# Perceiver block on one core: where the sums of the keys' squares stand, and in which tiles of TensorE they are made

## The chip, the core and the metric

The kernel runs on one core of one Trainium2 chip. The metric is the device time of one launch in microseconds (us). Five engines work on queues of their own: TensorE (PE in the profile, its weight loads PEld), VectorE (DVE), ScalarE (ACT), GpSimd (POOL) and SyncE (SP), which issues the DMAs. They wait for each other by semaphores.

## What is computed

Everything is float32. `x` has 128 rows of 512. Three residual steps follow each other: cross attention of `x` to a context of 12544 rows (16 heads of 32), self attention with block-scaled weights (16 heads of 128), and a mixture of 32 experts with a shared one. The change lies in the first step, cut here to what matters:

```python
def rms_norm(x, w, eps=1e-6):
    return x * jax.lax.rsqrt(jnp.mean(x * x, axis=-1, keepdims=True) + eps) * w

q     = rms_norm(linear(x, q_w, q_b), norm_q_w)
k     = rms_norm(linear(ctx_txt, k_w, k_b), norm_k_w)         # ctx_txt: rows 257 and on
v     = linear(ctx_txt, v_w, v_b)
k_img = rms_norm(linear(ctx_img, k_img_w, k_img_b), norm_k_img_w)   # ctx_img: rows 0 to 256
v_img = linear(ctx_img, v_img_w, v_img_b)
out = linear(attention(q, k, v) + attention(q, k_img, v_img), o_w, o_b)
```

A key is divided by the root of the mean of its 512 squares. The weight `norm_k_w` is folded into the queries, and the factor of one key, called `rinv` in the kernel, is applied to its scores.

## The kernel before

**Blocks and tiles.** The context is cut into 25 blocks. Block 0 is the image part (257 rows in tiles of 86, 86 and 85), blocks 1 to 24 are the text part with 512 rows each (511 in the last) in four tiles of 128. A tile is numbered `t`, its place in its block `j` (0 to 3). The text before and after says "pass j" for the work done at tile j.

**Software pipeline.** While the tiles of block b are attended to, keys and values of block b+1 are made by `step(b + 1, k)`, k from 1 to 7. These are the seven products of Strassen's scheme in Winograd's form for the keys (`kp`) and for the values (`vp`), each of eight matmul records of 128x256 (line 1078; a float32 matmul shows as two records). Their sums of context halves (`xs`) are made by GpSimd in `ctx_sums` (lines 1060 to 1063). Steps 1 and 2 share a bank of PSUM, as do 5 and 3, and 7 and 4. Three banks (pool `ps_a`) serve all these products and the `ssq` tiles below in turn.

**Per tile** the main loop (line 1523) does the following, and `pin` keeps each engine's instructions in the order of the program:

- `scores(t, "b")`: 16 matmuls in four groups of 32 rows into the four banks of `sb` (line 1162)
- `weights`: VectorE makes p = sb * rinv - maximum in one instruction over 128x2048 (line 1251), ScalarE its exponential (line 1259)
- `weigh_pending`: the 16 matmuls of the tile before, weights times values, in four groups of 32 columns (`av_new`, line 1268)
- `into_sums`: GpSimd adds the weights of the tile before to `ls` (line 1426), one instruction over 128x2048

**The squares.** When step 3 has filled the first half of a block's keys, ScalarE squares it (`squares(b, 0)`, line 1117), and GpSimd adds the four chunks of 128 channels into one by two instructions (`add_squares(b, 0)`, line 1123). Step 4 fills the second half, treated by `add_squares(b, 1)`. `key_norms(b, [0, 1])` and `key_norms(b, [2, 3])` then finish the sums for two tiles each: one matmul per tile with the squares as weights and a single column of ones (`ssq`, line 1015), one small VectorE instruction (`ms`, line 1025) and one power of -1/2 by GpSimd (`rinv`, line 818 through `inv_sqrt`).

**Order in a block of the main loop before the change**, for block b (what the change touches is in bold):

| pass | PE ahead of the scores | GpSimd | PE after `weigh_pending` |
|---|---|---|---|
| 0 | step 1 of b+1, **ssq of tiles 0 and 1 of b** | **rinv**, ls, squares (half 1) of b | step 2 |
| 1 | step 6, **ssq of tiles 2 and 3 of b** | **rinv**, ls | |
| 2 | step 5, step 7 of the keys | ls (and a weight scaling in six blocks) | step 3 |
| 3 | step 7 of the values | ls, **squares (half 0) of b+1**, xs of b+2 | step 4 |

The last block (24) has a sequence of its own from line 1628 on, and so have blocks 0 and 1, which end in a short loop over three tiles at line 1442. Between that loop and the main one GpSimd adds two small tensors (`x0ob`, `vbs`, lines 1467 and 1469).

Of the kernel before, what the change touches and what calls it, by code (L numbers as in the profile page):

```python
# [20 lines left out]
XH, XHD = 16, 32  # L21
# [749 lines left out]
def fast_block(ctx: ExitStack, tc: tile.TileContext, a: dict, out: bass.AP, amiss: bass.AP):  # L771
    nc = tc.nc
# [13 lines left out]
    ones = const.tile([P, P], FP, tag="ones", name="ones")  # L786
# [51 lines left out]
    def pin(ins):  # L838

        return tc.keep_in_program_order(ins)  # L840
# [55 lines left out]
    with ExitStack() as xs:  # L896
# [24 lines left out]
        m = -(-IMG // 3)  # L921
# [7 lines left out]
        NB, NT = len(blocks), len(tiles)  # L929
# [53 lines left out]
        sq = {}  # L983
# [26 lines left out]
        def key_norms(b, js):  # L1010

            ts = [blocks[b][3][j] for j in js]
            sp = bank(f"ssq_{b}_{js[0]}")
            for j, (o, m) in enumerate(ts):
                pin(nc.tensor.matmul(  # L1015
                    sp[:m, j : j + 1],
                    lhsT=sq[b][:, 0, o : o + m],
                    rhs=ones[:, 0:1],
                    start=True,
                    stop=True,  # L1020
                ))
            ms = small.tile([P, 4], FP, tag="ms", name=f"ms_{b}_{js[0]}")
            t0 = tile0[b] + js[0]
            for j0, j1, m in row_groups(ts):
                pin(nc.vector.tensor_scalar(  # L1025
                    ms[:m, j0:j1], sp[:m, j0:j1], 1.0 / D, 1e-6, ALU.mult, ALU.add
                ))
                pin(inv_sqrt(rinv[:m, t0 + j0 : t0 + j1], ms[:m, j0:j1]))
# [90 lines left out]
        def add_squares(b, i):  # L1119

            ks = slice(i * HALF, (i + 1) * HALF)
            for w in (2, 1):
                pin(nc.gpsimd.tensor_tensor(  # L1123
                    sq[b][:, :w, ks], sq[b][:, :w, ks], sq[b][:, w : 2 * w, ks], op=ALU.add
                ))
# [269 lines left out]
        m = heights[1]  # L1395
# [41 lines left out]
        def weigh_pending():  # L1437
            k, pk = pend
            weigh(k, pk, k in (t1, SWITCH), k == SWITCH - 1)


        for t in range(t1 + 1, tile0[2]):
            p, s = weights(t)
            j = t - t1
            if j == 1:
                largest(t, s)
                step(2, 6)
            elif j == 2:
                step(2, 5, "v")
                largest(t, s)  # L1450
            else:
                step(2, 7)
                largest(t, s)
                ctx_sums(3)
            weigh_pending()
            if j == 1:
                step(2, 5, "k")
            elif j == 2:
                step(2, 3)
            else:  # L1460
                step(2, 4)
            into_sums(*pend)
            if j == 2:
                add_squares(2, 0)
            pend = (t, p)
# [57 lines left out]
        for t in range(tile0[2], tile0[LAST]):  # L1523
            b, part, o, m = tiles[t]
            j = t - tile0[b]


            make = step
            if t == SWITCH + 3:
                pin(nc.tensor.matmul(  # L1530
                    avp["txt"].rearrange("p g q -> p (g q)"),
                    lhsT=ident,
                    rhs=kept["av"],
                    start=False,
                    stop=False,
                    skip_group_check=True,
                ))
            late = make if b + 1 < LAST else (lambda *of: None)
            if j == 0:
                make(b + 1, 1)  # L1540
                key_norms(b, [0, 1])
            elif j == 1:
                make(b + 1, 6)
                key_norms(b, [2, 3])
            elif j == 2:
                make(b + 1, 5)
                late(b + 1, 7, "k")
            else:
                late(b + 1, 7, "v")
            if t == tile0[LAST] - 1:  # L1550
                unsummed = pend
            else:
                into_sums(*pend)
            if j == 0:
                add_squares(b, 1)
            elif j == 2 and b in AHEAD:
                scale_weights((b - AHEAD[0]) // 3, "qkv"[(b - AHEAD[0]) % 3], nc.gpsimd)
            elif j == 3:
                add_squares(b + 1, 0)
                if b + 2 < NB:  # L1560
                    ctx_sums(b + 2)
            if t == SWITCH:
                m_bc["txt"] = m_new
            p, s = weights(t)
            weigh_pending()
            pend = (t, p)
            if t == tile0[RENEWED + 1]:
                m_new = xc.tile([P, 4, CHUNK], FP, tag="mx", name="mb_new")
                on_all(q_new, m_new, "new")
                pin(nc.vector.tensor_tensor(over, q_new, q_old, ALU.subtract))  # L1570
                less = small.tile([P, XH], FP, tag="less", name="less")
                pin(nc.scalar.activation(less, over, AF.Exp, scale=-1.0))
            elif t == tile0[RENEWED + 1] + 1:

                shrink = rowp.tile([P, D], FP, tag="h", name="shrink")
                on_heads(less, shrink, "less")
            elif t == SWITCH:
                av_old = avp["txt"].rearrange("p g q -> p (g q)")
                kept = {"av": row("kept_av", "kept_av")}
                pin(nc.vector.tensor_tensor(kept["av"], av_old, shrink, ALU.mult))  # L1580
                avp["txt"] = ps_o.tile([P, NC, P], FP, tag="o", name="av_new")
            elif t == SWITCH + 2:
                lp = bank("l_old")
                for i in range(4):
                    r = slice(i * XHD, (i + 1) * XHD)
                    pin(nc.tensor.matmul(
                        lp[r, :], lhsT=ones[:, :XHD], rhs=ls_old[i // 2][:, i % 2, :],
                        start=True, stop=True, skip_group_check=True,
                    ))
                kept["l"] = row("kept_l", "kept_l")  # L1590
                pin(nc.vector.tensor_tensor(kept["l"], lp, shrink, ALU.mult))
            if j == 2:
                make(b + 1, 3, "k")
            if b <= RENEWED:
                largest(t, s)
            if j == 0:
                make(b + 1, 2)
            elif j == 2:
                make(b + 1, 3, "v")
            elif j == 3:  # L1600
                late(b + 1, 4)
                if b + 3 < NB:
                    load_ctx(b + 3)
            if t == tile0[RENEWED + 1] - 1:
                q_new = query_max(mx, P, "t1")
            if b == RENEWED + 3 and j == 0:
                pin(nc.vector.reciprocal(l_img, l_img))
            if b == RENEWED + 3 and j == 1:
                flat = att_img.rearrange("p g q -> p (g q)")
                pin(nc.vector.tensor_tensor(flat, flat, l_img, ALU.mult))  # L1610
            if b == RENEWED + 3 and j == 2:
                pin(nc.gpsimd.tensor_tensor(
                    att_img, att_img, vbs.unsqueeze(2).to_broadcast([P, NC, P]), op=ALU.add
                ))
            if b == AHEAD[0] - 2 and j == 0:
                for t_, nm in ((bq, "bq"), (bk, "bk"), (gw, "gate_w")):
                    pin(nc.sync.dma_start(out=t_, in_=a[nm]))
                pin(nc.sync.dma_start(out=gb, in_=a["gate_bias"].partition_broadcast(P)))
                homes[2] = slot(xc, "mb", "q")
                load_codes(2, "q", homes[2][0])  # L1620
                load_codes(2, "k", homes[2][1])
            if b == AHEAD[0] - 1 and j == 0:
                for g in range(2):
                    for nm, t in zip("qkv", homes[g]):
                        load_codes(g, nm, t)
                    load_scales(g, aw.tile([P, 3 * GW], FP, tag="sc", name=f"sc_{g}"))

        b, t = LAST, tile0[LAST]
# [1 line left out]
        bo = rowp.tile([P, D], FP, tag="h", name="bo")  # L1630
        k, p = pend
        s = scores(t, "b")
        key_norms(b, [0, 1])
        ps = [weights(t, s, xc.tile([P, 4, CHUNK], FP, tag="vw", name="p_last"))[0]]
        step(b, 7, "k")
        step(b, 4, "k")
# [222 lines left out]
    for g in range(NG):  # L1859
# [17 lines left out]
        if g:  # L1877
            o = gather(g - 1)
# [35 lines left out]
    for q in range(4):  # L1914
        for k in range(4):
            j = 4 * q + k
            pin(nc.tensor.matmul(  # L1917
                yp,
                lhsT=aoT[:, j, :],
                rhs=wo[q][k // 2][:, k % 2 * D : k % 2 * D + D],  # L1920
                start=(j == 0),
                stop=(j == SH - 1),
# [351 lines left out]
    sp = {}  # L2274
# [175 lines left out]
```

## Time and profile before

| what | value |
|---|---|
| median of three runs | 1094.71 us (1092.88 to 1095.63) |
| the profiled execution, its own time | 1091.79 us |
| its span in the profile | 1090.1 us |
| granted clock of TensorE | 0.997 |
| PE busy | 1064.8 us (98%), 10464 matmul records |
| GpSimd busy | 691.0 us (63%) |
| VectorE, ScalarE busy | 545.6 us (50%), 356.1 us (33%) |
| one block of the main loop | 34.10 us |

The page shows the busy time of each engine, the span in 40 slices, and the chain of work that ended last, followed back from the end. The chain of waits gives the time that one step adds between its neighbours; the timeline gives start and length of each run of like instructions, where a matmul's length includes its passage through the array, so that lengths of neighbours overlap. "128*32" means weights with 128 rows and 32 columns.

### The profile page before, as it was taken

How to read it: one execution, taken by the hardware profiler on the slowest of the kernel's cores; microseconds unless marked ns; L12 is line 12 of the kernel's file. 1: busy time of each engine (PE TensorE's matmuls, PEld its weight loads, DVE VectorE, ACT ScalarE, POOL GpSimd, SP SyncE). 2: the span in 40 equal slices, each digit the busy share in tenths (PEclk: the TensorE clock that was granted, in tenths of full speed). 3: DMA queues.
4: the chain of work that ended last, by engine and by line, in shares of the span. 5: the costliest groups of instructions: out<-in, count | busy, mean ns of one | idle time of the engine just before them, and what ended most of it. 6: DMA issues, size and time to landing. Idle time of an engine off the chain costs nothing.

```text
span 1090.1 us, 23595 instructions
## 1 busy us (share of the span) xinstructions
PE 1064.8 (98%) x10464; PEld 844.3 (77%) x10464; DVE 545.6 (50%) x668; ACT 356.1 (33%) x438; POOL 691.0 (63%) x374
## 2 busy tenths in 40 slices
PE   8999999999999999999999999999999899999996
PEld 6778888888888888888888888888888669754332
DVE  3676864574445544455444554445544568441110
ACT  2353333333333333333333333333333324303111
POOL 2256886887878778787787888889888600000000
PEclk9999999999999999999999999999999999999999
DMA  9221021101111011110124201111010499519995
GB/s 307 90 79 41 2 88 40 41 1 40 40 40 41 2 40 40 40 41 2 40 82 165 59 2 40 40 40 40 1 41 1 141 390 368 174 72 413 384 414 234
DMA packets 43247, 113.17 MB, mean 104 GB/s; under 512 B 6720, under 2 KB 12032, under 8 KB 42112
## 3 DMA queue, kind: packets, MB, share of 16 engines
q1 hardware_dynamic: 43136, 111.57, 28.2%
q8 instruction: 84, 1.38, 0.5%
q14 instruction: 27, 0.22, 0.1%
HBM read 111.26 MB, written 0.29 MB: 102 GB/s over the span
## 4 chain that ended last, share of the span: by engine, by line
PE 89%; DVE 3%; DMA 3%; POOL 2%; ACT 1%; issue 1%; SPq 0%; DVEq 0%; ACTq 0%; POOLq 0%
PE kp L1078 27%; PE vp L1078 25%; PE sb L1162 10%; PE av_new L1268 8%; PE up L2075 4%; PE acc L2062 2%; PE ssq L1015 1%; PE qp L1759 1%; PE kp L1759 1%; PE yp L1917 1%; PE svp L1780 1%; PE vp L1230 1%; DMA h<-in_experts 1%; DMA wo<-in_experts 1%; DMA wv<-in_experts 1%; DVE p L1251 1%
## 5 line engine op out<-in xcount | busy, mean ns | idle before, releaser
L1426 POOL TENSOR_TENSOR ls<-ls,p 128x2048 f32<-128x2048 f32 x81 | 369.1, 4556 | 38.2 <-ACT p L1259 36.6
L1259 ACT ACTIVATE p<-p 128x2048 f32<-128x2048 f32 (+1 forms) x95 | 179.9, 1893 | 462.1 <-DVE p L1251 461.9
L1251 DVE SCALAR_TENSOR_TENSOR p<-sb,rinv,mb_new 128x2048 f32<-128x2048 f32 (+1 forms) x86 | 199.9, 2325 | 59.2 <-PE sb L1162 59.2
L1123 POOL TENSOR_TENSOR sq<-sq 128x512 f32<-128x512 f32 x96 | 96.2, 1002 | 33.1 <-ACT sq L1117 29.3
L1162 PE MATMUL sb<-qT_txt,kraw 32*128 32x128 f32 (+1 forms) x3040 | 111.5, 283 | 1.5 <-DVE p L1251 1.5
L1162 PEld LDWEIGHTS sb<-qT_txt,kraw 32*128 32x128 f32 (+1 forms) x3040 | 93.4, 186 | 19.6 <-issue 17.1
L1078 PE MATMUL kp<-xs,w_k_w 128*128 128x256 f32 x384 | 95.4, 392 | 0.0
L1078 PE MATMUL kp<-ctx,w_k_w 128*128 128x256 f32 x384 | 93.3, 386 | 0.0
L1078 PE MATMUL kp<-xs,kt 128*128 128x256 f32 x384 | 92.7, 385 | 0.1
L1268 PE MATMUL av_new<-p,v 128*32 128x128 f32 (+1 forms) x2720 | 92.5, 276 | 0.0
L1078 PE MATMUL vp<-vt,xs 128*128 128x256 f32 x384 | 91.1, 380 | 1.1 <-ACT kraw L1106 1.1
L1078 PE MATMUL vp<-w_v_w,xs 128*128 128x256 f32 x384 | 90.9, 380 | 0.0
L1078 PE MATMUL vp<-w_v_w,ctx 128*128 128x256 f32 x384 | 90.8, 380 | 0.0
L818 POOL TENSOR_TENSOR rinv<-ms,neghalf 128x2 f32<-128x2 f32 (+4 forms) x51 | 39.6, 778 | 71.2 <-DVE ms L1025 71.2
L1078 PEld LDWEIGHTS kp<-xs,kt 128*128 128x128 f32 x384 | 73.6, 193 | 11.4 <-POOL wk L1426 0.4
L1078 PEld LDWEIGHTS kp<-xs,w_k_w 128*128 128x128 f32 x384 | 69.3, 190 | 16.3 <-issue 8.9
L1078 PEld LDWEIGHTS vp<-vt,xs 128*128 128x128 f32 x384 | 72.8, 190 | 11.4 <-ACT kraw L1106 1.6
L1078 PEld LDWEIGHTS kp<-ctx,w_k_w 128*128 128x128 f32 x384 | 70.9, 190 | 13.7 <-issue 5.3
L1078 PEld LDWEIGHTS vp<-w_v_w,xs 128*128 128x128 f32 x384 | 72.9, 190 | 10.0
L1078 PEld LDWEIGHTS vp<-w_v_w,ctx 128*128 128x128 f32 x384 | 72.9, 190 | 9.8
L1268 PEld LDWEIGHTS av_new<-p,v 128*32 128x32 f32 (+1 forms) x2720 | 69.6, 110 | 11.2 <-issue 1.2
L818 POOL TENSOR_TENSOR rs_x<-ve_x,neghalf 128x1 f32<-128x1 f32 x3 | 1.7, 551 | 101.2 <-DVE ve_x L826 101.2
(441 smaller groups left out, 1470.4 us busy)
## 6 DMA issues: line engine op xcount, KB each, us to landing
ctx<-in_ctxT SPq DMA_DIRECT2D x23, 1024.0 KB, 4.9
wo<-in_experts SPq DMA_DIRECT2D x20, 512.0 KB, 9.9
wo<-in_wo_codes SPq DMA_DIRECT2D x8, 512.0 KB, 6.9
wq<-in_experts SPq DMA_DIRECT2D x8, 512.0 KB, 9.8
wk<-in_experts SPq DMA_DIRECT2D x8, 512.0 KB, 9.2
wv<-in_experts SPq DMA_DIRECT2D x8, 512.0 KB, 9.2
q<-in_experts SPq DMA_DIRECT2D x8, 512.0 KB, 9.4
f<-in_experts SPq DMA_DIRECT2D x8, 512.0 KB, 9.7
```

The costliest lines, as they stand in the source:

```text
L818: return nc.gpsimd.tensor_tensor(dst, src, neghalf[:m, :n], op=ALU.pow)
L1015: pin(nc.tensor.matmul(sp[:m, j : j + 1], lhsT=sq[b][:, 0, o : o + m], rhs=ones[:, 0:1], start=True, stop=True,))
L1078: pin(nc.tensor.matmul(t[:, h, :], lhsT=lhs, rhs=rhs, start=(first and h == 0 and c == 0), stop=(h == 1 and c == 1), skip_group_check=True,))
L1123: pin(nc.gpsimd.tensor_tensor(sq[b][:, :w, ks], sq[b][:, :w, ks], sq[b][:, w : 2 * w, ks], op=ALU.add))
L1162: pin(nc.tensor.matmul(s[:m, i, g * P : (g + 1) * P], lhsT=kraw[b][rows, g, o : o + m], rhs=qT[part][rows, g, :], start=True, stop=True,))
L1251: pin(nc.vector.scalar_tensor_tensor(p[:m, k : k + n], s[:m, k : k + n], rinv[:m, t : t + 1], m_bc[part][:m, k : k + n], ALU.mult, ALU.sub ...
L1259: pin(nc.scalar.activation(p[:m, k : k + n], p[:m, k : k + n], AF.Exp))
L1268: pin(nc.tensor.matmul(avp[part][i * XHD : (i + 1) * XHD, g, :], lhsT=vv[b][:m, t - tile0[b], hd * XHD : (hd + 1) * XHD], rhs=p[:m, i, g * ...
L1426: pin(nc.gpsimd.tensor_tensor(d, d, src, op=ALU.add))
L1759: pin(nc.tensor.matmul(pp[:, k, :], lhsT=w[:, c, k * SHD : (k + 1) * SHD], rhs=hT2[:, c, :], start=(c == 0), stop=(c == NC - 1),))
L2062: pin(nc.tensor.matmul(acc, lhsT=lhsT, rhs=rhs, start=(n_acc == 0), stop=last))
L2075: pin(nc.tensor.matmul(up[r : r + m, :], lhsT=lhsT, rhs=w13_of((kind != "all", i), c), start=(c == 0), stop=(c == NC - 1), skip_group_chec ...
```

## The change

The sums of squares of a tile are made by four matmuls, each with 32 columns of the weights into 32 rows of PSUM, in place of one with 128 columns. Both calls of `key_norms` of a block now stand after `weigh_pending`: that of tiles 2 and 3 still in pass 1, that of tiles 0 and 1 in pass 3 of the block before. For the latter `add_squares(b + 1, 0)` is moved ahead of `into_sums` of pass 3 on GpSimd. Block 2's first call moves to the last pass of the short loop, the last block's first call from its own sequence to the main loop. The calls of blocks 0 and 1 and the last block's second call stay where they are, in the new form.

```diff
@@ key_norms
             for j, (o, m) in enumerate(ts):
-                pin(nc.tensor.matmul(
-                    sp[:m, j : j + 1],
-                    lhsT=sq[b][:, 0, o : o + m],
-                    rhs=ones[:, 0:1],
-                    start=True,
-                    stop=True,
-                ))
+
+                for r in range(0, m, XHD):
+                    r1 = min(r + XHD, m)
+                    pin(nc.tensor.matmul(
+                        sp[r:r1, j : j + 1],
+                        lhsT=sq[b][:, 0, o + r : o + r1],
+                        rhs=ones[:, 0:1],
+                        start=True,
+                        stop=True,
+                        skip_group_check=True,
+                    ))
@@ short loop over the tiles of block 1
             weigh_pending()
+            if j == 3:
+                key_norms(2, [0, 1])
@@ main loop
             if j == 0:
                 make(b + 1, 1)
-                key_norms(b, [0, 1])
             elif j == 1:
                 make(b + 1, 6)
-                key_norms(b, [2, 3])
...
+            if j == 3:
+                add_squares(b + 1, 0)
             if t == tile0[LAST] - 1:
                 unsummed = pend
             else:
                 into_sums(*pend)
...
-            elif j == 3:
-                add_squares(b + 1, 0)
-                if b + 2 < NB:
-                    ctx_sums(b + 2)
+            elif j == 3 and b + 2 < NB:
+                ctx_sums(b + 2)
...
             p, s = weights(t)
             weigh_pending()
+            if j == 1:
+                key_norms(b, [2, 3])
+            elif j == 3:
+                key_norms(b + 1, [0, 1])
@@ last block
         s = scores(t, "b")
-        key_norms(b, [0, 1])
```

## The prediction

> **What bounds the kernel now.** I read the page first (busy time by engine), then the groups by shape, the chain of waits through one block, and the timeline of single instructions.
>
> ```profile
> PE 1064.8 (98%) x10464; PEld 844.3 (77%) x10464; DVE 545.6 (50%) x668; ACT 356.1 (33%) x438; POOL 691.0 (63%) x374
> ```
>
> ```profile
> L1268 PE MATMUL av_new<-p,v 128*32 128x128 f32 x2688 | 90.8, 276 | 0.0
> ...
> L1015 PE MATMUL ssq<-ones,sq 128*128 128x1 f32 x190 | 24.2, 231 | 0.8 <-POOL sq L1123 0.8
> ```
>
> In the main loop PE is never idle: over one block (520.6 to 554.7) its busy time is 34.10 of 34.10 us. So what a step adds on PE is what it costs, and the chain of waits gives that (columns: start, us, what):
>
> ```profile
> 520.42 0.34 PE ssq L1015 x4
> 520.75 1.10 PE sb L1162 x32
> 521.86 1.01 PE av_new L1268 x32
> 522.87 1.92 PE kp L1078 x8
> ```
>
> A call of key_norms for two tiles is four records and 0.34 us. A check without the chain: the scores of tiles 0, 1 and 2 start at 520.68, 530.24 and 537.73. The first distance, 9.56 us, holds 32 product records and one call, the second, 7.49, 24 records and none; eight records are 1.73 in the chain, so the call is 9.56 - 7.49 - 1.73 = 0.34. How the two forms run shows in the timeline (start, length of the whole run, engine, shape, count):
>
> ```profile
> 520.04 0.63 PEld L1015 LDWEIGHTS ssq<-ones,sq 128*128 128x128 f32 x4
> 520.25 0.50 PE L1015 MATMUL ssq<-ones,sq 128*128 128x1 f32 x4
> ```
>
> ```profile
> 521.79 0.16 PEld L1268 LDWEIGHTS av_new<-p,v 128*32 128x32 f32 x8
> ```
>
> ```profile
> 521.79 0.32 PE L1268 MATMUL av_new<-p,v 128*32 128x128 f32 x4
> ```
>
> A full load lasts 190 ns, one of 32 columns 110: 80 ns for 96 columns, so 0.83 ns a column, 107 ns for 128 and 27 for 32. Today's call is four loads of 107 of which the first lies under the product ahead: 3 x 0.107 = 0.32 of the 0.34. It is bound by loads, not by its single column. The av_new rows show what side by side means: eight loads of 110 ns end within 0.16 us, so they start within 0.05; four matmuls of 0.297 us end within 0.32, so they start within 0.02, some 7 ns apart.
>
> **The change part by part.** *The matmuls.* 44 calls (blocks 2 to 23, two each) leave the place ahead of the scores: -0.34 each. Each comes back after av_new as 16 pairs of load and matmul in the tile form in which av_new runs, so with no change of form ahead of it; the change to the full array behind it is paid today as well (kp after av_new: 1.92 against 1.73). Call the new price x. In each of four column groups there are four loads of 27 ns; the first hides under av_new's last stream as today's hides under vp; 3 x 27 plus the spread of 7 ns over four groups is 0.11. Ends: 0.10, and 16 times av_new's own pace (1.01/32 = 31.6 ns) = 0.51, an upper end because that pace streams 128 columns. I take 0.13, near the load rows, because the call of today is load-bound in the same sense. 44 x (0.13 - 0.345) = -9.5.
>
> Here a rule speaks against the change. The Trainium skill (TensorE: Matmul & The Clock Gate, section "Wait — 56ns, not 53.3ns?") says that starts of matmuls never come closer than about 25 ns however few columns stream, and its page TensorEngine Tiling (Array Packing), section "Instruction Overhead", advises not to tile a dimension that is small already, as one column costs like 60. By it x = 16 x 25 = 0.40, and the matmuls would give 44 x 0.055 = +2.4 in place of -9.5. The row above has four starts within 0.02 us, so the floor does not hold between column groups; whether it holds for 16 in a row no run here shows, since av_new's bursts pause for their streams. I follow the row, and keep 0.40 as a case.
>
> *What waits behind the new place.* The bank of tiles 2 and 3 is reused by step 7 (kp at 535.7), which now waits for ms; ms stands behind p on VectorE: 531.55 + 2.35 + 0.15 = 534.05, 1.6 us early. The bank of tiles 0 and 1 is reused by step 1 (550.68): p 546.53 + 2.35, ms at 549.04, also 1.6 early. The rinv of tiles 2 and 3 now stands behind the ls of pass 1, ends near 534.6 and is read at 539.04. All cost nothing; with less cover each 0.1 us would cost 2.2 in 22 blocks. No DMA is moved, and none is issued by these steps; SP's order stays.
>
> *GpSimd's order in pass 3*, the one place without cover:
>
> ```profile
> 543.24 1.04 ACT L1117 ACTIVATE sq<-kraw 128x1024 f32<-128x1024 f32 x1
> 543.48 4.54 POOL L1426 TENSOR_TENSOR ls<-ls,p 128x2048 f32<-128x2048 f32 x1 [2.73 <-ACT p L1259]
> ...
> 547.98 2.10 POOL L1123 TENSOR_TENSOR sq<-sq 128x512 f32<-128x512 f32 x2
> ...
> 555.18 0.70 POOL L818 TENSOR_TENSOR rinv<-ms,neghalf 128x2 f32<-128x2 f32 x1
> ...
> 556.12 2.35 DVE L1251 SCALAR_TENSOR_TENSOR p<-sb,rinv,mb_new 128x2048 f32<-128x2048 f32 x1 [1.07 <-PE sb L1162]
> ```
>
> From 543.48 to 555.88 GpSimd runs 12.40 us without a gap, and rinv is ready just ahead of p. With the squares first it cannot start before ScalarE's squares end, 544.28 (+0.08 as at 849.42 to 849.50 in the last block). The sums are then ready at 546.45, 0.9 us before av_new of pass 3 ends (547.34): PE does not wait for them. But rinv ends at 544.36 + 12.40 = 556.76, and p waits for it. What follows from a late rinv is in the trace already, at the start of block 2, where x0ob stands ahead of it:
>
> ```profile
> 108.52 0.66 POOL rinv L818
> ...
> 109.21 2.36 DVE p L1251
> ...
> 111.59 1.91 ACT p L1259
> 113.50 0.73 ACT kraw L1106 x2
> ...
> 114.28 1.99 PE vp L1078 x8
> ```
>
> vp of step 6 takes the bank that ScalarE's kraw frees, 5.07 us after p starts; there PE lost 1.15 us. In the loop: 556.76 + 0.04 + 5.07 = 561.87 is the earliest vp, less the 0.345 - x that PE gained in pass 1 ahead of those squares: 561.525 + x. PE alone would be there at 527.87 + 34.10 - 2(0.345 - x) = 561.28 + 2x. So PE stalls by 0.245 - x, 0.115 at x = 0.13, in 20 of the 22 blocks (the first two have longer VectorE stages): +2.3.
>
> *Edges.* At the start of block 2 rinv now stands ahead of ls, x0ob and vbs, so its stall goes: -1.15 (next late: ls, which has some 2 us before its p buffer is due). In the last block the path runs through the call:
>
> ```profile
> 853.53 0.55 PE ssq L1015 x4
> 854.10 0.17 DVE ms L1025
> ...
> 854.34 0.71 POOL rinv L818
> 855.08 2.36 DVE p_last L1251
> ```
>
> With rinv made before (squares 851.6, ms behind p at 852.5, rinv 853.2), p_last starts at the end of the scores, 853.6: -1.5; what is late next is the scores, which wait for the p before them. The last block's second call stays behind av_new: -0.2. Blocks 0 and 1 pay for changes of tile form between full-array work, about +0.2 (kp's 0.19) each where PE is on the path: +0.3.
>
> Sum: -9.5 + 2.3 - 1.15 - 1.5 - 0.2 + 0.3 = -9.7 us. Made against the profiled execution, 1091.8 (span 1090.1), it gives 1082.1; that run lies 2.9 under the median, so of the median 1094.7 it is 1085.0. Two runs' difference of about 0.3%, 3.3 us, is what the measurement can tell.
>
> **The rivals.**
> 1. *Sixteen small pairs run at av_new's sustained pace* (slower). If 31.6 ns is a limit of issuing and not of streaming 128 columns, x = 0.51: 44 x 0.16 = +7.0, edges -2.2, so +4.9: 1099.6. Decided at x = 0.40, where the loop's loss equals the edges' gain. For: nothing in the trace has more than eight short starts in a row. Against: starts 7 ns apart, and bursts of four with 0.11 us pauses, the length of a stream. Chance 0.12.
> 2. *The floor of 25 ns*, x = 0.40: +0.1, so 1094.8, no change. Chance 0.13.
> 3. *GpSimd's chain binds more than the rows add up to*: if rinv comes 0.3 later still, the loop gains 0.43 - 0.415 and the edges remain, about -2.3: 1092.4. For: the stall of block 2 is the same chain. Chance 0.10.
> 4. *x between*, about 0.25, with a pass of the same column group waiting for the one ahead: no stall, 44 x -0.095 = -4.2, edges -2.4: 1088.1. Chance 0.20.
> 5. *The forecast* with x from 0.10 to 0.17 (-10.5 to -8.8, or -12 if the stall does not appear). Chance 0.45.
> That the squares are still made ahead of the scores by a scheduler is no rival: the order of the built program puts eight ssq matmuls behind av_new on PE.
>
> **How the numbers follow.** The likeliest is 5: 1085.0. The low end is its no-stall case, 1082; the high end takes in 3 and most of 2: 1095. Faster by over 0.3%: 5, 4 and a third of 3, 0.68; within 0.3%: most of 2 and the rest of 3, 0.19; slower: 1 and a little of 2, 0.13.
>
> **What would show it.** Right: ssq in the chain near 0.1 us after av_new; kp after it still about 1.9; a block of 33.8; PE idle ahead of vp some 0.1 us with kraw as releaser; VectorE's p of pass 0 waiting for rinv; no p waiting for rinv near 109. Wrong: ssq at 0.4 or more, or kp behind it above 2.2; ssq waiting for GpSimd's sq; a block of 34.1 or longer with PE idle ahead of vp.

## The result and the profile after

| | before | after |
|---|---|---|
| median, us | 1094.79 (5 runs, 1092.88 to 1095.63) | 1080.82 (5 runs, 1080.05 to 1082.35) |
| ratio | | 0.9878, 95% interval 0.9865 to 0.9891 |
| profiled execution: own time, span | 1091.79, 1090.1 | 1080.82, 1079.1 |

The kernel became 14.0 us faster; the prediction was 1085.0, from 1082 to 1095. The direction and the mechanism were right, but the gain was larger than forecast: the time lies 1.2 us under the low end, so the prediction missed. With the later runs there are 46 of before, median 1093.5 (1091.85 to 1096.45), and 9 of after, median 1080.8: against this larger sample the gain is 12.7 us.

The page's busy times of after, and its groups by shape:

```profile
PE 1054.4 (98%) x11052; PEld 826.1 (77%) x11052; DVE 540.9 (50%) x668; ACT 356.0 (33%) x438; POOL 689.7 (64%) x374
```

```profile
L1272 PE MATMUL av_new<-p,v 128*32 128x128 f32 x2688 | 90.8, 276 | 0.0
...
L1018 PE MATMUL ssq<-ones,sq 128*32 128x1 f32 x778 | 13.9, 170 | 1.7 <-POOL sq L1127 1.7
```

PE has 588 records more and is busy for 10.4 us less: in a call of `key_norms`, 16 small pairs of a weight load and a matmul cost less than 4 large ones. (Lines have moved by 3 or 4: 1015 is now 1018, 1251 is 1255, 1268 is 1272.)

The chain of waits through a block (start, us, what) shows the call of `key_norms` behind av_new:

```profile
505.01 1.10 PE sb L1166 x32
506.12 0.99 PE av_new L1272 x30
507.11 0.11 PE ssq L1018 x15
507.22 1.92 PE kp L1082 x8
...
521.82 1.80 PE vp L1082 x8
```

av_new and ssq together take 1.10 us where av_new alone took 1.01; kp behind them takes 1.92 as before. vp of step 6 takes 1.80 in place of 1.73: that is the stall that was predicted. Its cause is in the timeline (start, length, engine, what; in brackets the engine's idle time before it and its releaser):

```profile
504.11 2.07 POOL L1127 TENSOR_TENSOR sq<-sq 128x512 f32<-128x512 f32 x2 [3.96 <-ACT sq L1121]
506.14 4.56 POOL L1430 TENSOR_TENSOR ls<-ls,p 128x2048 f32<-128x2048 f32 x1
...
515.82 0.70 POOL L818 TENSOR_TENSOR rinv<-ms,neghalf 128x2 f32<-128x2 f32 x1
...
516.55 2.35 DVE L1255 SCALAR_TENSOR_TENSOR p<-sb,rinv,mb_new 128x2048 f32<-128x2048 f32 x1 [4.95 <-POOL rinv L818]
```

GpSimd waits for ScalarE's squares, then runs without a gap, and p of pass 0 waits for its rinv.

The two waits for rinv at the edges are gone. First the chain at the start of block 2, where vp now follows kp at once, then in the last block, where p_last follows the scores (before, it came at 855.08, behind ssq, ms and rinv, while the scores had started at 852.36):

```profile
111.31 1.73 PE kp L1082 x8
113.04 0.02 issue
113.06 1.99 PE vp L1082 x8
...
842.07 1.22 PE sb L1166 x32
...
843.38 0.06 DVE p_last L1255
```

Where the time went, from the starts of the scores and of later matmuls in both traces:

| stretch | before, us | after, us | difference |
|---|---|---|---|
| start to the scores of tile 7 | 105.57 | 105.48 | -0.09 |
| tile 7 to 11 (block 2) | 37.71 | 36.07 | -1.65 |
| tile 11 to 19 | 70.53 | 69.47 | -1.06 |
| tile 19 to 91, 18 blocks | 613.74 | 606.43 | -7.31 (-0.406 each) |
| tile 91 to 95 | 24.80 | 24.62 | -0.18 |
| tile 95 to the output projection | 30.00 | 28.05 | -1.95 |
| from there to the gate's matmul | 83.49 | 83.49 | 0.00 |
| gate to the end | 124.22 | 125.48 | +1.26 |

All that the change touches gives -12.24 us. A second profile of the changed kernel gives only -11.35 up to the output projection: in block 3 VectorE waits 1.36 us there for the landing of a small DMA (`shrink`), and PE 0.81 us behind it. That DMA belongs to both kernels and lands late in five of the twelve profiles, the split at the old place among them, so such an account is good to about 1 us. The last row has the experts' transfers; other profiles show below how far it moves by itself.

### The profile page after: what moved, and what is told of

Its sections match the earlier page's. It is cut to its first block, busy times and chain, and to the rows that moved or that the text cites. A ratio compares the mean times of both kernels' runs of the same rounds, so it can differ in the third digit from the quotient of the medians.

```text
span 1079.1 us, 24731 instructions
## 1 busy us (share of the span) xinstructions
PE 1054.4 (98%) x11052; PEld 826.1 (77%) x11052; DVE 540.9 (50%) x668; ACT 356.0 (33%) x438; POOL 689.7 (64%) x374
## 4 chain that ended last, share of the span: by engine, by line
PE 91%; DMA 3%; DVE 3%; issue 1%; ACT 1%; POOL 0%; SPq 0%; DVEq 0%; ACTq 0%
PE kp L1082 28%; PE vp L1082 26%; PE sb L1166 10%; PE av_new L1272 8%; PE up L2082 4%; PE acc L2069 2%; PE qp L1766 1%; PE kp L1766 1%; PE yp L1924 1%; PE svp L1787 1%; PE vp L1234 1%; DMA wv<-in_experts 1%; DMA wo<-in_experts 1%; DMA h<-in_experts 1%; PE av_old L1272 1%
## 5 line engine op out<-in xcount | busy, mean ns | idle before, releaser
L1121 ACT ACTIVATE sq<-kraw 128x1024 f32<-128x1024 f32 x48 | 50.0, 1042 | 12.1 <-DVE kraw L1112 12.1
```

Source lines behind the costliest of these rows:

```text
L1121: pin(nc.scalar.activation(sq[b][:, :, ks], kraw[b][:, :, ks], AF.Square))
```

## The experiments

**The split alone.** It is made at the old place ahead of the scores; the rest is as before.

```diff
-                pin(nc.tensor.matmul(
-                    sp[:m, j : j + 1],
-                    lhsT=sq[b][:, 0, o : o + m],
+                for r in range(0, m, XHD):
+                    r1 = min(r + XHD, m)
+                    pin(nc.tensor.matmul(
+                        sp[r:r1, j : j + 1],
+                        lhsT=sq[b][:, 0, o + r : o + r1],
```

> The kernel before with its ssq matmuls split into four groups of 32 columns, at the old place ahead of a tile's scores; GpSimd's order is the old one. Theory A (the price of a call is its loads, plus a change of tile form where its neighbours have another form): a call costs 0.10 us as after av_new, plus a change of form on one side that the full-array call did not pay there, some 0.1 to 0.19 us (0.19 is what kp pays behind av_new, 1.92 against 1.73). So 0.20 to 0.29 us a call in place of 0.345, a block of 33.8 to 34.0 us, 44 calls give -6.4 to -2.4 us, and no edge of the other parts: 1088.4 to 1092.4. Theory B (the split alone does it, the place is indifferent): 0.10 a call, 44 x -0.245 = -10.8: about 1084. Theory C (the place does it, the split is worth nothing): 0.34 a call, 1094.8.

Measured 1089.76 us, ratio 0.9956 (0.9942 to 0.997) to the kernel before, measured beside it, as in all that follow. The chain of waits:

```profile
516.79 1.73 PE vp L1082 x8
518.52 0.24 PE ssq L1018 x16
518.75 1.10 PE sb L1166 x32
```

A call takes 0.24 in place of 0.34, a block 33.89. That is theory A's range: the split alone brings 0.10 a call, and the place is not indifferent.

**The place alone.** The changed kernel with the 128-column matmul of before.

```diff
-                for r in range(0, m, XHD):
-                    r1 = min(r + XHD, m)
-                    pin(nc.tensor.matmul(
-                        sp[r:r1, j : j + 1],
-                        lhsT=sq[b][:, 0, o + r : o + r1],
+                pin(nc.tensor.matmul(
+                    sp[:m, j : j + 1],
+                    lhsT=sq[b][:, 0, o : o + m],
```

> The changed kernel with the ssq matmuls of 128 columns on the whole array, as before, but at the new places behind av_new, and with GpSimd's new order. Theory A: three loads of 107 ns stand open, 0.32 us, and the change of form (0.19) moves from kp to ssq, so ssq with kp costs 0.34 more than kp alone, as today: the loop gains nothing from PE, no stall ahead of vp (0.245 - 0.345 is below nothing), and the edges stay (block 2 about -1.2, last block about -1.9): 1091 to 1092, block 34.10 us. Theory C (the place does it): near 1082. A form change that is paid twice would show as ssq above 0.45 or kp still at 1.92 behind it, and 1095 or more.

Measured 1093.49 us, ratio 1.0 (0.9992 to 1.0009), between theory A's 1092 and the 1095 of a form change that is paid twice. The chain of waits:

```profile
531.87 1.01 PE av_new L1268 x32
532.88 0.54 PE ssq L1015 x4
533.42 1.83 PE kp L1078 x8
```

ssq and kp take 2.37, kp alone 1.92, so the call costs 0.45 here, and a block is 34.31. My theory was off by 0.11, one load of 107 ns: behind av_new the first full load is not covered either. By single records the four loads start 0, 108, 217 and 329 ns behind the first, and kp's first load 441 ns behind it. The new place alone is worse for the loop; what its edges give (block 2, the last block) pays for most of that, -3.1 us against +4.2 in this trace.

Taken from the lengths of blocks, the four prices of a call of two tiles are:

| us a call | ahead of the scores | behind av_new |
|---|---|---|
| 128 columns | 0.345 | 0.453 |
| four groups of 32 | 0.243 | 0.105 |

The two parts do not add up: the move costs 0.11 with the old form and gains 0.14 with the new one.

**GpSimd's old order.** The changed kernel, with the squares' sums of pass 3 behind ls.

```diff
-            if j == 3:
-                add_squares(b + 1, 0)
             if t == tile0[LAST] - 1:
...
-            elif j == 3 and b + 2 < NB:
-                ctx_sums(b + 2)
+            elif j == 3:
+                add_squares(b + 1, 0)
+                if b + 2 < NB:
+                    ctx_sums(b + 2)
```

> The changed kernel with GpSimd's old order in pass 3 alone: the squares of the first half are added up behind the sums of the weights (ls, 4.54 us) instead of ahead. Theory A: ls starts when p's exponentials are there, some 0.6 us ahead of ScalarE's squares, the squares are then done about 2.7 us after av_new of pass 3 has ended, and PE, whose ssq stands behind av_new, waits that long in some 21 blocks: +50 to +60 us against the changed kernel, near 1135, and PE's idle time in front of ssq names GpSimd's sq. Theory D (GpSimd's order is free because PE's queue has slack): within 3 us of the changed kernel.

Measured 1177.51 us, ratio 1.076 (1.0738 to 1.0781): 96.7 us over the changed kernel, far over both theories. PE's waits (engine, line, releaser: us in total, times, longest) give the part that was foreseen:

```profile
PE ssq L1018 <- POOL sq L1127: 56.4, 22, 2.9
```

Two of the 22, 1.7 us together, stand at calls outside the loop, at 55 us and in the last block, as in the changed kernel. The other 20 are 2.73 us each. The rest is in the chain behind one of these waits, and in the busy times by stretch (stretch, its length, then the engines' busy times; the third last column is the granted clock):

```profile
594.81 0.39 PE ssq L1018 x16
595.21 3.71 PE kp L1082 x8
598.91 2.90 PE vp L1082 x8
```

```profile
594.80:598.90 4.10, 4.09 (x25) 3.36 (x26) 0.16 (x1) 0.70 (x1) 3.94 (x4) 0.50 0.02 4
598.90:601.80 2.90, 2.90 (x10) 2.36 (x9) 0.88 (x2) 1.06 (x1) 2.90 (x3) 0.61 0.00 0
601.80:612.00 10.20, 10.20 (x103) 8.64 (x102) 3.04 (x2) 4.25 (x6) 6.29 (x4) 1.00 0.70 216
```

kp takes 3.71 in place of 1.92 at a granted clock of 0.50. The trace has 0.50 behind 18 of the 20 waits, for 3.4 us behind 12 of them and for 6.8 us behind six, of which this is one; behind the first two waits (135 and 210 us) the clock stayed at 1.00. A block is 38.68, 4.99 more than in the changed kernel: 2.73 of waiting and some 2.25, on average, of what follows it, nearly all of it the slow array. So the third part of the change, four moved lines on GpSimd, is what makes the new place usable at all.

**rinv ahead of the context sums.** The changed kernel with xs of pass 3 behind the call of `key_norms`.

```diff
-            elif j == 3 and b + 2 < NB:
-                ctx_sums(b + 2)
...
             elif j == 3:
                 key_norms(b + 1, [0, 1])
+                if b + 2 < NB:
+                    ctx_sums(b + 2)
```

> The changed kernel with the four sums of the context (xs, 4.8 us on GpSimd) of pass 3 behind the reciprocal roots of the next block's first tiles instead of ahead of them. Theory A (the late rinv delays p of pass 0, that ScalarE's kraw, that the bank of vp of step 6: 0.07 to 0.08 us a block): rinv is ready some 4 us ahead of p, p waits for the scores alone, vp of step 6 takes 1.73 again, a block is 33.61 us and 20 blocks give 1.4 to 1.6 us: about 1079.3. Theory E (vp's 1.80 is something else, such as the form of the work ahead): rinv is early but the block stays at 33.69, 1080.8. If xs then comes late for step 6 or 5, PE idles there and it is slower.

Measured 1078.92 us, ratio 0.9857 (0.9841 to 0.9872), block 33.617. The group of p by shape, first of after and then of this run (instructions, busy, mean ns of one, idle before it and what ended it):

```profile
L1255 DVE SCALAR_TENSOR_TENSOR p<-sb,rinv,mb_new 128x2048 f32<-128x2048 f32 x84 | 197.5, 2351 | 128.5 <-POOL rinv L818 93.9 <-PE sb L1166 24.0 <-POOL sq L1127 10.6
```

```profile
L1255 DVE SCALAR_TENSOR_TENSOR p<-sb,rinv,mb_new 128x2048 f32<-128x2048 f32 x84 | 197.5, 2351 | 110.5 <-PE sb L1166 99.8 <-POOL sq L1127 10.6
```

rinv no longer ends a wait of p. The stall is gone: 0.074 us a block, theory A. The loads in the timeline show why it was no more than that, first in after:

```profile
519.72 1.70 PEld L1082 LDWEIGHTS kp<-xs,kt 128*128 128x128 f32 x8
521.63 1.38 PEld L1082 LDWEIGHTS vp<-vt,xs 128*128 128x128 f32 x7 [0.21 <-ACT kraw L1110]
```

and with rinv early, load and matmul of the same vp:

```profile
522.06 1.70 PEld L1082 LDWEIGHTS vp<-vt,xs 128*128 128x128 f32 x8
522.28 1.89 PE L1082 MATMUL vp<-vt,xs 128*128 128x256 f32 x8
```

A load starts 0.21 us ahead of its matmul and needs only 0.107 of that, so it can be some 0.107 late at no cost. From ScalarE's squares to this load are 18.63 us in after and 18.45 here (medians of 18 blocks): the load came 0.18 late, 0.107 of that was covered, and 0.073 was left. Single records agree: behind the late load the next one starts after 0.108 us, behind a punctual one after 0.216.

**Four times the pairs.** On the version with rinv early, each matmul of the sums is issued four times.

```diff
-                for r in range(0, m, XHD):
+                for r in [r for _ in range(4) for r in range(0, m, XHD)]:
```

> The kernel of the run with rinv ahead of the context sums (the base, 1078.9 us, block 33.62), with every ssq matmul issued four times over: 64 small pairs in a row in place of 16, the same sums. It measures the price of a pair in a long row. Loads of one column group in series, four groups at once: 12 more loads of 27 ns in each group, +0.32 us a call, 44 calls give +14; starts 7 ns apart give +0.34, +15, so 1093 to 1094, block 34.26 to 34.30. A floor of 25 ns between starts that the first 16 escape through some queue: 48 x 25 ns = +1.2 us a call, +53: about 1132. av_new's pace of 31.6 ns: +67, about 1146.

Measured 1099.22 us, ratio 1.0057 (1.0041 to 1.0072), block 34.49: 0.437 us for 48 pairs more, 9.1 ns a pair. That is neither the floor of 25 ns that the prediction had weighed nor av_new's 31.6, but more than the 7 of the forecast. The timeline has all 64 loads and matmuls in:

```profile
517.45 0.74 PEld L1018 LDWEIGHTS ssq<-ones,sq 128*32 128x32 f32 x64
517.56 0.72 PE L1018 MATMUL ssq<-ones,sq 128*32 128x1 f32 x64
```

By single records, bursts of four matmuls start 31 ns apart at first (107, 136, 167, 199 ns behind the first load); from about the 24th pair on, a pair starts every 16.7 ns, 67 for four. The short call of the change ends before that slower pace begins. What sets it was not tested.

**Two groups of 64 columns.** The same version, with wider groups.

```diff
-                for r in range(0, m, XHD):
-                    r1 = min(r + XHD, m)
+                for r in range(0, m, 2 * XHD):
+                    r1 = min(r + 2 * XHD, m)
```

> The same base with two groups of 64 columns in place of four of 32: 8 pairs a call. It tells the two readings of 0.10 us apart, since 4 loads of 27 ns in series and 16 starts 7 ns apart are the same number there. Loads bind (the groups load at the same time): each group has four loads of 53 ns, 0.21 us or 0.16 with the first hidden, so a call costs 0.06 to 0.11 more and a block 33.74 to 33.84, 1081.5 to 1084. Starts bind: 8 x 7 ns = 0.06, a block of 33.54, 1077. If the groups load one after the other: 8 x 53 ns = 0.43, 34.26, 1093.

Measured 1088.84 us, ratio 0.9965 (0.9951 to 0.9978), block 34.078: none of the three numbers. A call costs 0.231 more than with four groups. The loads in the timeline, first of the changed kernel, then of this one:

```profile
506.04 0.81 PEld L1272 LDWEIGHTS av_new<-p,v 128*32 128x32 f32 x32
506.83 0.30 PEld L1018 LDWEIGHTS ssq<-ones,sq 128*32 128x32 f32 x16
```

```profile
529.44 0.81 PEld L1272 LDWEIGHTS av_new<-p,v 128*32 128x32 f32 x32
530.45 0.31 PEld L1018 LDWEIGHTS ssq<-ones,sq 128*64 128x64 f32 x8 [0.20 <-issue]
```

The loads themselves take as long (0.31 and 0.30). But they begin 1.01 us after av_new's first load and not 0.79: groups of another width than av_new's start 0.20 us after av_new's last load has ended, as the whole array does in the run with the place alone (the same 0.20 of idle). Within the call, pairs of loads start 57 ns apart (0, 55, 111, 169): about a load of 64 columns at 0.83 ns, with the two groups at the same time. With four groups of 32 the distance is about 30 ns, with the whole array 108. So within a call loads bind and groups run side by side; the forecast had left out the change of form.

**The kernel before, once more.**

> The kernel before once more, for a second profile: the first one's profiled execution (1091.8) lies below all of the 24 other runs (1092.1 to 1096.5). If the difference sits in the loop, a block here is longer than 34.10 us; if it sits in the last stages with their large transfers, the stretch from the gate's matmul to the end is longer than 124.2 us (it was 124.4 to 125.5 in the other kernels' profiles) at a block of 34.10; if it is the clock, the granted clock after the last block's idle time is lower.

Measured 1093.29 us, 1.5 more than the first profiled execution. A block is 34.097 us, the same as in the first, and the stretch from the gate to the end is 124.41. 1.2 of the 1.5 us are behind the output projection, in the busy times of 880 to 900 us (first profile, then this one; granted clock third from the end):

```profile
880.00:900.00 20.00, 17.77 (x138) 14.30 (x129) 15.28 (x29) 2.96 (x13) 0.55 (x1) 1.00 1.01 394
```

```profile
880.00:900.00 20.00, 17.98 (x126) 13.70 (x123) 13.97 (x27) 2.16 (x9) 0.55 (x1) 0.91 1.01 394
```

It is the clock: here it is 0.50 for 3.4 us from 884.0 on. The loop has no part in it. The first profile has such a stretch too, from 854.2 on in the last block; there PE would have waited for p_last anyway, and it costs 0.1 us (30.00 us from tile 95 to the output projection, 29.89 here). So the gain in the last block is not a matter of the clock. Over all profiles the stretch from the output projection to the gate is 83.5 or 84.7 us, and the one from the gate to the end 124.1 to 125.5, whatever the kernel.

**Squares between two halves of ls.** On the version with rinv early, GpSimd does half of ls, the squares, and the other half.

```diff
+            if j == 3 and t != tile0[LAST] - 1:
+                half_sums(*pend, 0)
             if j == 3:
                 add_squares(b + 1, 0)
...
+            elif j == 3:
+                half_sums(*pend, 1)
```

> The same base with GpSimd's ls of pass 3 in two halves (2.27 us each), the first ahead of the squares' sums and the second behind. It makes PE wait for a short time: the squares are done about 0.6 to 0.8 us after av_new. In the run with the squares behind all of ls, each wait of 2.6 us was followed by a stretch at a granted clock of 0.5 to 0.6 that cost 2.4 us more. If any wait brings the clock down: 22 x (0.7 + up to 2.4), 1110 to 1147. If only long ones do: 22 x 0.7 = +15, near 1094, with kp behind ssq at 1.92.

Measured 1094.66 us, ratio 1.0018 (1.0008 to 1.0027), block 34.383. PE's waits and the chain:

```profile
PE ssq L1018 <- POOL sq L1127: 12.9, 22, 0.9
```

```profile
548.98 0.31 PE ssq L1018 x16
549.28 1.92 PE kp L1082 x8
```

Without the same two calls outside the loop, a wait of 0.56 us is paid once a block, and ssq takes 0.31 in place of 0.12, since its first load is no longer covered: 0.75 a block by these two, 0.77 by the blocks. kp keeps 1.92, and the clock stays at 1.00 in all 20 blocks. A wait of 0.56 us did not bring the clock down; 18 of the 20 waits of 2.73 us did.

**Both versions side by side.** The changed kernel and the one with rinv early are measured once more, both unchanged.

> The changed kernel once more, beside the version with rinv ahead of the context sums, on one chip. Its gain against before was 14.0 us against five runs of before and would be 12.5 against the 39 of the later calls, whose median is nearer 1093.3. If the first sample of before lay high, the ratio here is 0.988 to 0.990 (-11 to -13 us); the traces' own account up to the last projection of the attention is -12.24 us.

> The version with rinv ahead of the context sums once more, against the changed kernel in the same call. Theory A: 20 blocks x 0.073 us = 1.5 us under the changed kernel. Rival: the 1.9 us between the two calls was the chips' or the last stages' scatter (stretches of 124.1 to 125.5 us in the traces), and the two are alike within 0.5 us.

Measured 1080.69 us, ratio 0.9884 (0.9867 to 0.99), and 1079.56 us, ratio 0.988 (0.9862 to 0.9898). The blocks repeat their 33.69 and 33.62 us. By the trace the version with rinv early is 18 x 0.073 = 1.3 us ahead over those blocks alone; the pooled medians (1080.8 of 9 runs, 1079.3 of 8) agree, but the intervals of these two measurements do not part them. It is the best version here by its blocks, not by a time that stands clear of the scatter.

## Why the prediction was right in kind and short in size

- **The price of a call** (44 x (0.13 - 0.345) = -9.5). It is load-bound with groups side by side, as argued; the size was 0.105, so -10.6. The step that failed: I rounded 0.11 up to 0.13 without a row for it. This term is short by 1.1 us, the largest part of the miss. The floor of 25 ns between starts (the Trainium skill, TensorE: Matmul & The Clock Gate, "Wait — 56ns, not 53.3ns?"), which I weighed and did not follow, does not hold here between column groups: the first four matmuls of the call start 108, 114, 121 and 128 ns behind its first load, 16 pairs fit into 0.105 us, and 64 still average under 10 ns.
- **The stall ahead of vp** (+2.3). The chain was right link by link: from ScalarE's squares to p 13.56 us were predicted and measured, and vp's load starts 5.07 after p. The step that failed is "PE stalls by 0.245 - x": it charged all of the load's lateness. With the measured x it gives 0.14; the load came 0.18 late, and as a load normally runs 0.21 ahead and needs only 0.107, the stall was 0.074 in 20 blocks, +1.5. Short by 0.8.
- **Edges.** Block 2: -1.15 predicted; the stretch lost 1.65, of which two calls are 0.48, so -1.17. From tile 91 on, the prediction's terms are two calls (-0.43), -1.5 and -0.2, together -2.13; the lengths give -2.13, or -2.02 against the second profile of before. That it is exact to the last figure is luck. The +0.3 for blocks 0 and 1 is not there: in the chain of block 0 the call fell from 0.39 to 0.29 us and the vp behind it rose from 3.52 to 3.61, and the whole stretch is -0.09. Short by about 0.4.
- **What hides the rest** (ms, the banks of step 7 and step 1, ls): nothing of it appears in PE's waits. Right.
- **The sum.** With measured sizes, the terms give -10.6 for the calls, +1.5, -1.2 for block 2 and -1.7 for the last block without its calls, which is -12.0; the two traces of the changed kernel have -12.24 and -11.35 up to the output projection.
- **The low end** of 1082 was the no-stall case with x = 0.13. It took -12 from a median of three runs, 1094.7, that lay 1.2 us above the 1093.5 of 46, which made the range too high by as much. From 1093.5 the sum -12.2 gives 1081.3, within half a microsecond of what was measured; that the first trace had no late DMA in block 3 helps there.
- **Rivals.** 16 pairs at av_new's pace (x = 0.51), the floor (0.40) and the case between (0.25) fall with x = 0.105. "GpSimd's chain binds more" fell, but its place was right: the run with the squares behind ls shows what is a few instructions away. The forecast named no case of a lowered clock, which adds 2.25 us a block there to the wait itself.
- **The tail.** The 1.26 us that after gives back from the gate on is mostly scatter: the second profile of the same kernel has 124.82 us there in place of 125.48, the version with rinv early 124.6 in both of its profiles. Whether the rest, some 0.5 us against before's 124.22 and 124.41, belongs to the change is not shown.

## What to carry to other kernels

The small matmuls were cheap where their neighbour already ran in the same groups of the array, 0.105 us a call, and more than twice as dear at the other place: price the form change with the edit, since the same move cost 0.11 us with one form and gained 0.14 with another. When work is moved ahead in one engine's queue, follow the chain of the engine that feeds it; here GpSimd's order decided between -14 and +83 us. And when charging a late bank or buffer, first take off the lead that a prefetched load has.

## What the runs showed of the hardware that was not expected

- Behind 18 of 20 waits of PE of 2.73 us the granted clock was 0.50, for 3.4 or 6.8 us, which cost nearly as much again (2.25 us a block); 20 waits of 0.56 us left it at 1.00. The Trainium skill (TensorE: Matmul & The Clock Gate, "HAM oscillation — how this bites in real kernels") names gaps of more than about 3.4 us; here 2.73 were enough. The length of one wait does not decide alone: in the last block of before, the first profile has 0.50 from 854.2 on behind a wait of 1.53 us, and the second, with the same wait, has 1.00.
- Groups of 64 columns behind groups of 32 cost a change of form like the whole array: in both, the first load begins 0.22 us later than in groups of 32.
- In a row of 64 small pairs a pair started every 8 ns at first, and every 16.7 ns after some 24 pairs.
